# A hybrid attention and spectral-filter kernel: a short first chunk beside the front's last steps, the residual stored in raster order by ScalarE, and the chunks kept in written order

## The chip, the cores and the metric

The kernel runs on one core of one Trainium2 chip. The metric is the device time of one execution in microseconds (us). The engines are TensorE (PE, with PEld for its weight loads), VectorE (DVE), ScalarE (ACT), GpSimd (POOL) and SyncE (SP). SP only issues DMAs; ACT and POOL issue DMAs too, beside their other work.

## What is computed

The input is four images of 56 x 56 tokens with 128 channels, all in float32.

1. Layer 0: layer norm, 7 x 7 neighbourhood attention with four heads, projection with residual, layer norm, an MLP (128 to 512 to 128, GELU) with residual.
2. Layer 1, on the 3136 tokens of each image: a token-wise norm `t`, then `t + q * sum(k * v)`.
3. Layer 1, second half, on the norm `u` of that result: a residual plus a gated sum of spectral filters. Each filter is a causal convolution over tokens, followed by a 128 x 128 matrix per filter (16 filters, with and without an alternating sign), plus a short autoregressive part over three lags:

```python
U = irfft(rfft(phi) * rfft(u)); out = einsum('btkd,k,kde->bte', U_plus, s, Mpp)
out = out + einsum('btkd,k,kde->bte', U_minus, s, Mpm)     # filters
out = out + sum(u shifted by i @ Mu[i] for i in range(3))  # autoregressive part
```

The kernel does the convolution in the frequency domain with 8 x 245 frequencies: it transforms tokens to spectra, multiplies each frequency by a 128 x 128 matrix, and transforms back.

## The kernel before

The kernel has three stages that follow one another.

**The front** (to about 1255 us) takes the images in turn. The attention of image b (28 small tiles, `step`) is interleaved with the dense work of image b-1 (`finish_image`), by written costs: each `yield` names what a piece costs, and `dense` is advanced until a due amount is spent. The order on each engine's queue is that of the program text, since the whole front stands in `tc.manual_schedule()`. For the last image there is no attention left; its `finish_image` is interleaved only with `matrices`, which loads 32 blocks of filter matrices (512 KB each, line 992) and sums them into `mc`.

`finish_image` ends so: for each quarter j of the tokens, eight matmuls `px` (line 686) with wave tables `tab` (loaded by SP, line 298, five or ten ahead) give spectra, which DVE and POOL combine into `ab`; POOL stores `ab` to the scratch tensor `ud` (line 710). `last_steps` then does, for each of seven row groups g, `recent(g)` (the autoregressive part: matmuls `par`, line 628, and a DVE add into `x`, line 636) and `residual(g-1)` (four transposes `pf`, line 644, an ACT copy to `xf`, line 647, and four stores to `xd` from SP, line 650). For images 0 to 2 `last_steps` is spread over the quarters; for the last image all of it comes after them.

**The chunks** (about 1266 to 1816 us) multiply frequencies by matrices. There are 31 chunks of 8 x 8 frequencies; 245 = 30 x 8 + 5, so the last has five in place of eight. Chunk c needs

- `tokens(c)`: a 1 MB load `xc` from `ud` (line 1035), and 19 operations on POOL (`evens`, six; `odds`, ten; then two sums and a negation, lines 1047 to 1049) that make its spectra `v`. In chunk 0 the six evens are DVE's;
- `make(c, u)` for u = 0 to 7: 16 matmuls `pg` (line 1071, two records each) and four copies into the matrix tile `g` of 64 KB per partition, two on ACT (line 1082) and two on DVE (line 1084);
- `product(c, part)` for part = 0 to 7: matmuls `py` (line 1102) of `g` with `v`; after parts 1 and 5 ACT copies a sum to `ya`, after parts 3 and 7 DVE makes two `ys` and SP stores them to `yd` (line 1121).

The loop of chunk c alternates `make(c+1, u)` with `product(c, u)`. `xc`, `v` and `g` have two buffers each. This stage stands outside `manual_schedule`: the framework's scheduler orders the instructions of each queue by its own estimate of time. In the program that it made, SP's queue holds the `xc` loads of chunks 1, 2 and 3 ahead of chunk 0's stores, and from there on the load of chunk c+3 ahead of the stores of chunk c.

The pools of the chunks (`wg` with both `g`, `w3` with `xc`, `v` and the rest) are opened after `front.close()`, in the memory of the front.

**The back** (about 1808 to 2010 us) loads the products from `yd` into two `ring` tiles (in `g`'s buffers, 64 loads of 512 KB), combines them on DVE, multiplies them with inverse wave tables (`pi`, line 1219), adds the residual from `xd` and stores the result.

The lines by which the change can be followed: 101 (`qkv0`), 613 to 656 (`spread`, `recent`, `residual`, `last_steps`), 664 to 717 (`ab`, the quarters), 990 to 1025 (`matrices` and its interleaving), 1028 to 1169 (the chunks).

Of the kernel before, what the change touches and what calls it, by code (L numbers as in the profile page):

```python
# [25 lines left out]
GT = GR * W  # L26
QC = 14
# [22 lines left out]
NCH = -(-R // FC)  # L50
FB = 4
# [7 lines left out]
def conv_attn_hybrid_kernel(ctx: ExitStack, tc: tile.TileContext, a: dict, out: bass.AP):  # L59
# [11 lines left out]
    fp = front.enter_context(tc.tile_pool(name="front", bufs=1))  # L71
    attention = ExitStack()
# [4 lines left out]
    order = tc.manual_schedule()  # L77
    front.enter_context(order)
# [25 lines left out]
    qkv0 = load(fp, "qkv0", [C, 3 * C], a["w_qkv"], tag="xf", bufs=2)  # L104
# [84 lines left out]
    def setup_loads():  # L189
# [6 lines left out]
        late["fc10"] = load(fp, "fc10", [C, HID], a["w_fc1"], q, tag="xf", bufs=2)  # L196
# [4 lines left out]
        wl0 = fp.tile([C, 3, C], FP, tag="xf", name="wl0", bufs=2)  # L201
# [103 lines left out]
    def evens(eng, e, y, out):  # L305
        def all_of(v):
            last = " ".join("nf"[: len(v.shape) - 3])
            return v.rearrange(f"c p r {last} -> c (p r) {last}")

        eng.tensor_tensor(all_of(e[:, :2]), all_of(y[:, :2]), all_of(y[:, 2:]), ALU.add)  # L310
        eng.tensor_tensor(e[:, 2], y[:, 0], y[:, 2], ALU.subtract)
        eng.tensor_tensor(e[:, 3, 0], y[:, 3, 1], y[:, 1, 1], ALU.subtract)
        eng.tensor_tensor(e[:, 3, 1], y[:, 1, 0], y[:, 3, 0], ALU.subtract)
        if len(e.shape) > 4:
            e = e.rearrange("c p r n f -> c p r (n f)")
        eng.tensor_tensor(out[:, :2], e[:, ::2], e[:, 1::2], ALU.add)
        eng.tensor_tensor(out[:, 2:], e[:, ::2], e[:, 1::2], ALU.subtract)
# [181 lines left out]
    def finish_image(b, own=None):  # L499
# [118 lines left out]
        for r in range(2):  # L618
            spread(r, f"u{b}", rs, scale)
            yield 0.25  # L620
        def recent(g):
# [3 lines left out]
            for c0, c1 in zip(cuts, cuts[1:]):  # L625
# [9 lines left out]
            xg = raster(x[:, g])  # L635
            nc.vector.tensor_tensor(
                xg, ps[:, :GT].rearrange("c (h t w) -> c h t w", h=GR, t=NQ), xg, ALU.add
            )

        def residual(g):  # L640

            pf = ps_s.tile([TQ, NQ, C], FP, tag="s", name=f"pf_{b}_{g}")
            for t in range(NQ):
                nc.tensor.transpose(pf[:, t, :], x[:, g, t * TQ : (t + 1) * TQ], ident)
            tag, bufs = ("tok", 3) if own else ("xf", 2)
            xf = fp.tile([TQ, NQ, C], FP, tag=tag, name=f"xf_{b}_{g}", bufs=bufs)
            nc.scalar.copy(xf, pf)
            rows_of = xd[b].rearrange("(g h t w) c -> g t h w c", g=NG, h=GR, t=NQ)
            for t in range(NQ):
                nc.sync.dma_start(rows_of[g, t], xf[:, t, :])  # L650
# [14 lines left out]
        abs_of = (ab, own.tile([C, NCH, PH, 2 * FC], FP, name="ab2") if own else ab)  # L665
# [48 lines left out]
        if b == B - 1:  # L714
            yield from last_steps(range(NG))
# [264 lines left out]
    weighed = ExitStack()  # L980
    mpool = weighed.enter_context(tc.tile_pool(name="matrices", bufs=1, side="right"))
# [25 lines left out]

    with tc.tile_pool(name="last", bufs=1, side="right") as own, tc.tile_pool(
        name="weigh", bufs=1, side="right"
    ) as wp:  # L1010
        extra, due = matrices(wp), 0.0
        for spent in finish_image(B - 1, own):
            due += 0.4 * (spent if spent != "step" else 0.5)
            while due >= 1:
                next(extra, None)
                due -= 1
        run(extra)
    front.close()

    gpool = ctx.enter_context(tc.tile_pool(name="wg", bufs=2))
    with tc.tile_pool(name="w3", bufs=2) as wp, tc.tile_pool(
        name="ps_g", bufs=6, space=PSUM
    ) as ps_g, tc.tile_pool(name="ps_y", bufs=2, space=PSUM) as ps_y:
        filters_in, made, spectra, sums = {}, {}, {}, {}
        many = [min(FC, R - FC * c) for c in range(NCH)]

        def tokens(c):  # L1030


            n = NP * B
            x = wp.tile([C, n, CW], FP, tag="xc", name=f"xc{c}")
            (nc.sync if c else nc.gpsimd).dma_start(
                x, ud.rearrange("j b c w -> c (j b) w")[:, :, CW * c : CW * (c + 1)]
            )
            y = x.rearrange("c n (p r f) -> c p r n f", r=2, f=FC)
            v = wp.tile([C, 3, n * FC, PH], FP, tag="v", name=f"v{c}")
            w = v[:, 1:].rearrange("c r k m -> c m r k")  # L1040
            gp = nc.gpsimd
            ev = wp.tile([C, 4, 2, n, FC], FP, tag="od", name=f"ev{c}", bufs=1)
            evens(gp if c else nc.vector, ev, y[:, :4], w[:, :4])
            od = wp.tile([C, 3, 2, 2, n, FC], FP, tag="od", name=f"od{c}", bufs=1)
            odds(gp, od, y[:, 4:])
            od = od.rearrange("c i p r n f -> c i p r (n f)")
            gp.tensor_tensor(w[:, 4:6], od[:, 0], od[:, 2], ALU.add)
            gp.tensor_tensor(w[:, 6:], od[:, 0], od[:, 2], ALU.subtract)
            gp.tensor_scalar(v[:, 0], v[:, 2], -1.0, 1.0, ALU.mult, ALU.mult)
            spectra[c] = v  # L1050

        def filters_of(k):

            t = wp.tile([C, FB * CW], FP, tag="ph", name=f"ph{k}")
            n = min(FB, NCH - FB * k) * CW
            for rg in range(4):
                (nc.scalar if k else nc.gpsimd).dma_start(
                    t[32 * rg : 32 * rg + 32, :n], pd[:, FB * CW * k : FB * CW * k + n]
                )
            filters_in[k] = t  # L1060

        def make(c, u):

            if u == 0:
                made[c] = gpool.tile([C, CW, C], FP, tag="g", name=f"g{c}")
            g, t, at = made[c], filters_in[c // FB], c % FB * CW
            banks = [ps_g.tile([C, 4, CW], FP, tag="g", name=f"pg_{c}_{u}_{i}") for i in range(4)]
            for q in range(4):
                for rg in range(4):
                    r = slice(32 * rg, 32 * rg + 32)  # L1070
                    nc.tensor.matmul(  # L1071
                        banks[rg][:, q, :],
                        mc[r, 4 * u + q, :],
                        t[r, at : at + CW],
                        start=True,
                        stop=True,
                    )
            for rg in range(4):
                into = g[:, :, 32 * rg + 4 * u : 32 * rg + 4 * u + 4]
                src = banks[rg].rearrange("c q n -> c n q")  # L1080
                if rg % 2:
                    nc.scalar.copy(into, src)  # L1082
                else:
                    nc.vector.tensor_copy(into, src)  # L1084

        def weights(v, r, f, m):

            return v[:, r : r + 2].rearrange("c r (n f) m -> c f m (r n)", f=FC)[:, f, m]

        def product(c, part):  # L1090

            v, g = spectra[c], made[c]
            f0 = part // 4 * 4
            h, last = part // 2 % 2, min(many[c], f0 + 4)
            if part % 2 == 0:
                sums[0] = ps_y.tile([C, 4, C], FP, tag="y", name=f"py_{c}_{part}")
            py, f1 = sums[0], f0 + part % 2 * 2
            for f in range(f1, min(f1 + 2, last)):
                for r in range(2):
                    for m in range(4):  # L1100
                        slot = SLOTS.index(4 * h + m)
                        nc.tensor.matmul(  # L1102
                            py[32 * m : 32 * m + 32, f - f0, :],
                            weights(v, 1 - r, f, slot),
                            g[:, (2 * slot + r) * FC + f, :],
                            start=(r == 0),
                            stop=(r == 1),
                        )
            if part % 2 == 0:
                return  # L1110

            k = last - f0
            if h == 0:
                sums[1] = wp.tile([C, 4, C], FP, tag="ya", name=f"ya_{c}_{part}", bufs=1)
                nc.scalar.copy(sums[1][:, :k], py[:, :k])
                return
            for i, op in enumerate((ALU.add, ALU.subtract)):
                ys = wp.tile([C, 4, C], FP, tag=f"ys{i}", name=f"ys_{c}_{part}_{i}")
                nc.vector.tensor_tensor(ys[:, :k], sums[1][:, :k], py[:, :k], op)
                at = FC * c + f0  # L1120
                nc.sync.dma_start(yd[i, at : at + k, :C].rearrange("f q e -> q f e"), ys[:, :k])

        ring, ready, waves_back = [], {}, {}
        PAIR = 2 * B * C

        def ring_tile():
            name = f"ring{len(ring)}"
# [277 lines left out]
```

## Time and profile before

| | |
|---|---|
| median of 3 runs | 2007.86 us (2003.68 to 2009.82) |
| the profiled execution, its own time | 2011.93 us |
| its span | 2010.1 us |
| PE busy | 1854.4 us, 92% |
| DVE, ACT, POOL busy | 1201.5, 1029.0, 904.2 us |
| granted PE clock, mean | 0.953 |
| by stage, PE busy | 300 to 400: 92.95 of 100; 1260 to 1280: 10.62 of 20; 1400 to 1500: 100 of 100 |
| moved by DMA | 223.42 MB, mean 111 GB/s |

A line of the timeline gives start, duration, engine, source line, operation, output<-input tile, size and count; in square brackets stands the idle time before it and what ended it. "SPq" and "ACTq" are DMA issues on these engines' queues. A line of waits gives who waited for whom, the total, how often and the longest. A line of windows gives the stretch, then the busy time of PE, PEld, DVE, ACT and POOL, the granted PE clock, the busy share of the DMA engines and GB/s.

### The profile page before, as it was taken

The page shows a single profiled execution, that of the slowest core. Times are in us where ns is not written, and L with a number is a line of the kernel's source. Part 1 is how long each engine was busy: PE and PEld are TensorE (multiplying, and loading weights), DVE is VectorE, ACT ScalarE, POOL GpSimd, SP SyncE. Part 2 cuts the span into 40 slices and gives each one's busy share as a digit, 9 for nine tenths or more (in the row PEclk, how much of TensorE's full clock was granted, in tenths as well). Part 3 has the DMA queues.
Part 4 walks back from the last instruction along what each step waited for, and adds up shares of the span by engine and source line. Part 5 has one row for each costly group of instructions (what it writes and reads, how often), then busy time and mean ns, then how long its engine had stood idle before and what let it go on. Part 6 is the DMA issues. An engine that isn't in the chain of part 4 may idle for free.

```text
span 2010.1 us, 56713 instructions
## 1 busy us (share of the span) xinstructions
PE 1854.4 (92%) x23666; PEld 1172.5 (58%) x23666; DVE 1201.5 (60%) x2749; ACT 1029.0 (51%) x2311; POOL 904.2 (45%) x1446
## 2 busy tenths in 40 slices
PE   6899999998999988999998988699999999996998
PEld 3555554554554554554554434688888888882333
DVE  3676545454545554545555664577777777775883
ACT  1566685654686554685555333355555555550000
POOL 2444322564323463223473026588877777770000
PEclk8799999998999898999899989799999999997999
DMA  4140000153000252000254538344444444439991
GB/s 114 33 130 12 1 1 1 53 190 110 1 1 1 73 193 86 1 1 1 80 171 145 188 100 279 98 135 129 134 132 124 121 125 132 124 88 372 373 325 65
DMA packets 191389, 223.42 MB, mean 111 GB/s; under 512 B 12008, under 2 KB 171049, under 8 KB 188540
## 3 DMA queue, kind: packets, MB, share of 16 engines
q1 hardware_dynamic: 182992, 166.69, 27.3%
q0 software_dynamic: 2752, 34.33, 4.4%
q10 hardware_dynamic: 5388, 18.76, 2.6%
q8 instruction: 187, 3.06, 0.7%
q14 instruction: 70, 0.57, 0.1%
HBM read 141.77 MB, written 77.97 MB: 109 GB/s over the span
## 4 chain that ended last, share of the span: by engine, by line
PE 75%; issue 7%; DVE 6%; DMA 5%; ACT 4%; SPq 2%; POOL 1%; ACTq 0%; POOLq 0%; DVEq 0%
PE pg L1071 14%; PE py L1102 13%; PE pi L1219 7%; PE px L686 5%; PE ppt L794 4%; PE pl L738 4%; PE ph L537 3%; PE pf L528 3%; PE par L628 3%; PE pav L850 2%; PE pv L814 2%; DMA ring<-yd 2%; ACT p L765 2%; DVE p L751 2%; SPq L650 2%
## 5 line engine op out<-in xcount | busy, mean ns | idle before, releaser
L778 POOL TENSOR_SCALAR p<-p,den 112x280 f32<-112x280 f32 x448 | 214.9, 498 | 493.6 <-DVE den L776 264.9
L1084 DVE COPY g<-pg 128x512 f32<-128x512 f32 x496 | 319.5, 687 | 159.7 <-PE pg L1071 149.4
L1082 ACT COPY g<-pg 128x512 f32<-128x512 f32 x496 | 271.2, 602 | 235.7 <-PE pg L1071 228.6
L1071 PE MATMUL pg<-ph,mc 32*128 32x128 f32 x7936 | 298.9, 286 | 11.8 <-POOL od L326 5.1
L1071 PEld LDWEIGHTS pg<-ph,mc 32*128 32x128 f32 x7936 | 251.1, 189 | 52.7 <-issue 36.0
L765 ACT ACTIVATE p<-p,low 112x280 f32<-112x280 f32 x448 | 231.1, 517 | 92.3 <-DVE low L751 92.0
L1102 PE MATMUL py<-g,v 128*32 128x128 f32 x7840 | 275.2, 281 | 2.4 <-issue 2.0
L1102 PEld LDWEIGHTS py<-g,v 128*32 128x32 f32 x7840 | 219.1, 152 | 31.8 <-issue 2.9
L751 DVE CUSTOM_DVE_ANT_0 p<-pl,bias 112x280 f32<-112x280 f32 x448 | 174.7, 445 | 15.7 <-PE pl L738 3.5
L686 PE MATMUL px<-tab,tok 98*128 98x496 f32 x256 | 126.5, 638 | 21.0 <-DMA tab<-in_tab 14.1
L801 DVE COPY pt<-ppt 120x448 f32<-120x448 f32 x112 | 69.4, 620 | 117.4 <-PE ppt L794 116.5
L794 PEld LDWEIGHTS ppt<-ident,p 112*120 112x120 f32 x896 | 100.5, 139 | 59.4 <-issue 41.7
L794 PE MATMUL ppt<-ident,p 112*120 112x112 f32 x896 | 127.1, 263 | 5.7 <-DVE middle L836 4.3
L1219 PE MATMUL pi<-ring,io 128*98 128x512 f32 x256 | 112.9, 602 | 17.6 <-DVE ring L1181 15.5
L694 POOL TENSOR_TENSOR ab<-ab,w 128x496 f32<-128x496 f32 x60 | 74.5, 1242 | 108.4 <-ACT w L693 97.2
L801 ACT COPY pt<-ppt 120x448 f32<-120x448 f32 x224 | 87.1, 443 | 55.5 <-PE ppt L794 55.3
L537 PE MATMUL ph<-ln_m,w_fc 128*128 128x448 f32 x224 | 105.7, 564 | 4.7 <-DVE ln_m L518 4.6
L738 PE MATMUL pl<-kt,qt 32*112 32x280 f32 x896 | 94.0, 442 | 10.8 <-ACT qt L488 6.0
L545 ACT ACTIVATE h<-ph,b_fc 128x448 f32<-128x448 f32 x112 | 69.4, 633 | 61.8 <-PE ph L537 60.7
L528 PE MATMUL pf<-h,w_fc 128*128 128x448 f32 x224 | 101.0, 541 | 0.0
L686 PEld LDWEIGHTS px<-tab,tok 98*128 98x128 f32 x256 | 50.1, 207 | 79.3 <-issue 53.2
L1219 PEld LDWEIGHTS pi<-ring,io 128*98 128x98 f32 x256 | 42.6, 168 | 87.4 <-issue 80.9
(237 smaller groups left out, 3230.3 us busy)
## 6 DMA issues: line engine op xcount, KB each, us to landing
ring<-yd SPq DMA_DIRECT2D x64, 512.0 KB
ud<-ab POOLq DMA_DIRECT2D x16, 1984.0 KB, 7.1
yd<-ys SPq DMA_DIRECT2D x122, 256.0 KB
xc<-ud SPq DMA_DIRECT2D x30, 1024.0 KB
tab<-in_tab SPq DMA_DIRECT2D x160, 189.9 KB
mat<-in_M_phi_plus SPq DMA_DIRECT2D x16, 512.0 KB
mat<-in_M_phi_minus SPq DMA_DIRECT2D x16, 512.0 KB
x<-in_x SPq DMA_DIRECT2D x28, 224.0 KB
```

The lines of the kernel that those rows point to most:

```text
L537: nc.tensor.matmul(ph[:, :GT], w_fc1[:, i * C : (i + 1) * C], lnm[:, g * GT : (g + 1) * GT], start=True, stop=True,)
L686: nc.tensor.matmul(ps, toks[i // 4][:, i % 4, :], next(tab), start=True, stop=True)
L738: nc.tensor.matmul(pls[h][:TQ, :KEYS], qts[b, g][hs, t * TQ : (t + 1) * TQ], kt[hs, r0 : r0 + KR, c0 : c0 + KC], start=True, stop=True,)
L751: nc.vector.tensor_tensor_reduce(out=f["p"][:, h, :], in0=f["pls"][h][:TQ, :KEYS], in1=bias[:, h, :], scale=-1.0, scalar=3.0e38, op0=ALU.a ...
L765: nc.scalar.activation(f["p"][:, h, :], f["p"][:, h, :], AF.Exp, bias=f["low"][:, h : h + 1], scale=-1.0, accum_out=f["den"][:, h : h + 1],)
L778: nc.gpsimd.tensor_scalar(f["p"][:, h, :], f["p"][:, h, :], f["den"][:, h : h + 1], 1.0, ALU.mult, ALU.mult)
L794: nc.tensor.transpose(ppt[:, i, :], of, ident[:TQ, :TQ])
L1071: nc.tensor.matmul(banks[rg][:, q, :], mc[r, 4 * u + q, :], t[r, at : at + CW], start=True, stop=True,)
L1082: nc.scalar.copy(into, src)
L1084: nc.vector.tensor_copy(into, src)
L1102: nc.tensor.matmul(py[32 * m : 32 * m + 32, f - f0, :], weights(v, 1 - r, f, slot), g[:, (2 * slot + r) * FC + f, :], start=(r == 0), stop ...
L1219: nc.tensor.matmul(banks[j, p], it, z, start=(fh == 0 and k == 0), stop=(fh == 1 and k == len(of) - 1),)
```

## The change

- `residual(g)` no longer works on the (strip, row, column) order of `x`. `recent(g)` adds into a new tile `xr` in raster order (one of the three "t" buffers); `residual` transposes every fourth column of it, so that a partition of `xf` holds four tokens that follow each other, and one DMA from ACT's queue stores the group (2 KB per partition) in place of four from SP's. `xf` and the three weight tiles that shared its tag move to a pool `residual` of their own, opened after the front's; for the last image, too, it has two buffers (three of `tok` before).
- The three missing frequencies go to the first chunk in place of the last: chunk 0 uses frequencies 3 to 7 of its eight, `make(0, u)` computes 80 columns in place of 128, and `product` of the last chunk is full. The host's table is shifted to match.
- The pool of the chunks, `w3`, is opened on the right side, where `last` and `weigh` were, before the front's last steps of the last image. The filter load and `tokens(0)` are started there: `xc0` is loaded by SP in two parts (quarters 0 to 2, then 3), and DVE's evens are placed after `recent(5)` and `recent(6)`. DVE also takes one sum and the negation (in two parts) of chunk 0. The two `ab` tiles of the last image change places, so that the last quarter's is the front's.
- `g`'s two buffers become two pools of one buffer. `matrices` stays open to the end, and one inverse wave table of the back lies in `mc`.
- The last chunk's `ys` are stored by ACT in place of SP. `matrices` is advanced at 0.45 in place of 0.4 per unit of cost.
- `manual_schedule` now ends after the chunks: their instructions stand on each queue in the order of the program text.

The core of the diff:

```diff
+XQ = GT // TP
+SKIP = NCH * FC - R
...
+    res = front.enter_context(tc.tile_pool(name="residual", bufs=2))
...
-    order = tc.manual_schedule()
-    front.enter_context(order)
+    order = ExitStack()
+    order.enter_context(tc.manual_schedule())
...
+        xr = {}
+
         def recent(g):
...
-            xg = raster(x[:, g])
+            xr[g] = temp(f"xr_{b}_{g}")
             nc.vector.tensor_tensor(
-                xg, ps[:, :GT].rearrange("c (h t w) -> c h t w", h=GR, t=NQ), xg, ALU.add
+                xr[g].rearrange("c (h t w) -> c h t w", h=GR, t=NQ),
+                ps[:, :GT].rearrange("c (h t w) -> c h t w", h=GR, t=NQ),
+                raster(x[:, g]),
+                ALU.add,
             )
 
         def residual(g):
 
-            pf = ps_s.tile([TQ, NQ, C], FP, tag="s", name=f"pf_{b}_{g}")
-            for t in range(NQ):
-                nc.tensor.transpose(pf[:, t, :], x[:, g, t * TQ : (t + 1) * TQ], ident)
-            tag, bufs = ("tok", 3) if own else ("xf", 2)
-            xf = fp.tile([TQ, NQ, C], FP, tag=tag, name=f"xf_{b}_{g}", bufs=bufs)
+            pf = ps_s.tile([TP, XQ, C], FP, tag="s", name=f"pf_{b}_{g}")
+            for t in range(XQ):
+                nc.tensor.transpose(pf[:, t, :], xr[g][:, t::XQ], ident)
+            xf = res.tile([TP, XQ, C], FP, tag="xf", name=f"xf_{b}_{g}", bufs=2)
             nc.scalar.copy(xf, pf)
-            rows_of = xd[b].rearrange("(g h t w) c -> g t h w c", g=NG, h=GR, t=NQ)
-            for t in range(NQ):
-                nc.sync.dma_start(rows_of[g, t], xf[:, t, :])
+            nc.scalar.dma_start(
+                xd[b, g * GT : (g + 1) * GT].rearrange("(n t) c -> n t c", t=XQ), xf
+            )
             if b + 2 < B:
                 fetch(b + 2, [g])
...
-        abs_of = (ab, own.tile([C, NCH, PH, 2 * FC], FP, name="ab2") if own else ab)
+        abs_of = (own.tile([C, NCH, PH, 2 * FC], FP, name="ab2") if own else ab, ab)
...
         if b == B - 1:
+            yield "spectra"
             yield from last_steps(range(NG))
...
+        if c:
+            nc.sync.dma_start(x, src)
+        else:
+
+            nc.sync.dma_start(x[:, : n - B], src[:, : n - B])
+            nc.sync.dma_start(x[:, n - B :], src[:, n - B :])
+            yield
...
+        gp, other = nc.gpsimd, nc.gpsimd if c else nc.vector
...
+        yield from evens(other, ev, y[:, :4], w[:, :4])
+        yield
+        if c:
+            od = cp.tile(of, FP, tag=tag, name=f"od{c}", bufs=bufs)
+        odds(gp, od, y[:, 4:])
+        od = od.rearrange("c i p r n f -> c i p r (n f)")
+        other.tensor_tensor(w[:, 4:6], od[:, 0], od[:, 2], ALU.add)
+        gp.tensor_tensor(w[:, 6:], od[:, 0], od[:, 2], ALU.subtract)
+        for m in (slice(PH),) if c else (slice(4), slice(4, PH)):
+            other.tensor_scalar(
+                v[:, 0, :, m], v[:, 2, :, m], -1.0, 1.0, ALU.mult, ALU.mult
+            )
...
+        k, n = (FC - SKIP, 2 * PH * (FC - SKIP)) if c == 0 else (CW, CW)
+        of = t[:, at : at + CW]
+        if c == 0:
+            of = of.rearrange("k (x f) -> k x f", f=FC)[:, :, SKIP:]
...
+            (nc.scalar if c == NCH - 1 else nc.sync).dma_start(
+                yd[i, at + skip : at + 4, :C].rearrange("f q e -> q f e"), ys[:, skip:]
+            )
...
-        for spent in finish_image(B - 1, own):
-            due += 0.4 * (spent if spent != "step" else 0.5)
+        for spent in last:
+            if spent == "spectra":
+                break
+            due += 0.45 * (spent if spent != "step" else 0.5)
...
+    cp = chunks.enter_context(tc.tile_pool(name="w3", bufs=2, side="right"))
+    filters_of(0)
+    first = tokens(0)
+    next(first)
+    for n, _ in enumerate(last):
+        if n in (2 * NG - 5, 2 * NG - 3):
+            next(first, None)
+    run(first)
     front.close()
...
+    gpools = [ctx.enter_context(tc.tile_pool(name=f"wg{i}", bufs=1)) for i in range(2)]
+    ps_g = chunks.enter_context(tc.tile_pool(name="ps_g", bufs=6, space=PSUM))
+    ps_y = chunks.enter_context(tc.tile_pool(name="ps_y", bufs=2, space=PSUM))
+    for u in range(8):
+        make(0, u)
+    for c in range(NCH):
+        if c + 1 < NCH:
+            if (c + 1) % FB == 0:
+                filters_of((c + 1) // FB)
+            run(tokens(c + 1))
...
+        for u in range(8):
+            if c + 1 < NCH:
+                make(c + 1, u)
+            product(c, u)
+    chunks.close()
+    order.close()
...
-    full[..., :R] = tab
+    full[..., SKIP:] = tab
```

## The prediction, made before the change was run

> **What bounds the kernel now.** I read the windows by stage, then the order of PE's work at the seam between front and chunks, then the waits there, then one chunk on every queue. All times are of the profiled execution. Windows (PE, PEld, DVE, ACT, POOL busy; PEclk; DMA share; GB/s):
>
> ```profile
> 1260.00:1280.00 20.00, 10.62 (x136) 9.35 (x136) 6.81 (x12) 4.46 (x9) 16.85 (x26) 0.50 0.43 111
> 1400.00:1500.00 100.00, 100.00 (x2971) 86.90 (x2965) 73.33 (x118) 57.26 (x105) 79.76 (x109) 1.00 0.48 133
> ```
>
> In the chunks PE has no gap at all; a better order there can win nothing and can only lose. At the seam PE is half idle at half clock. PE's timeline there:
>
> ```profile
> 1254.43 0.60 PE L644 MATMUL pf<-ident,x 128*112 128x128 f32 x4
> 1259.86 1.10 PE L644 MATMUL pf<-ident,x 128*112 128x128 f32 x4 [4.83 <-DVE x L636]
> 1266.04 3.78 PE L1071 MATMUL pg<-ph,mc 32*128 32x128 f32 x48 [5.08 <-POOL od L326]
> 1273.71 3.78 PE L1071 MATMUL pg<-ph,mc 32*128 32x128 f32 x52 [3.89 <-ACT g L1082]
> ...
> 1288.04 1.16 PE L1071 MATMUL pg<-ph,mc 32*128 32x128 f32 x28 [0.57 <-DVE g L1084]
> 1289.13 1.12 PE L1102 MATMUL py<-g,v 128*32 128x128 f32 x32
> ```
>
> Waits at the seam (total, times, longest), and in the chunks:
>
> ```profile
> DVE g L1084 <- DMA xd<-xf: 10.3, 1, 10.3
> POOL v L316 <- PE py L1102: 84.5, 27, 3.5
> ```
>
> The first copy into `g0` waits for the residual stores, because `g0` lies where `xf` lay; SP issues the 28 stores until 1270.7. The second line is the important one: in the chunks POOL waits for PE, so spectra are made ahead of need. One chunk on POOL and SP:
>
> ```profile
> 1403.25 1.34 POOL L310 TENSOR_TENSOR ev<-xc 128x512 f32<-128x512 f32 x1
> ...
> 1409.15 1.33 POOL L316 TENSOR_TENSOR v<-ev 128x512 f32<-128x512 f32 x1 [3.05 <-PE py L1102]
> ...
> 1419.48 1.04 POOL L1049 TENSOR_SCALAR v<-v 128x1024 f32<-128x1024 f32 x1
> 1409.85 0.95 SPq L1121 DMA_DIRECT2D yd<-ys  x2
> 1414.93 0.36 SPq L1035 DMA_DIRECT2D xc<-ud  x1
> ```
>
> A chunk's last product ends at E = 1408.91. POOL then writes the `v` of two chunks on and is done at 1420.49, E + 11.6; PE wants it at E + 18.4 (a chunk of 17.3, (1807.8 - 1305.3)/29, and the 1.1 of one `pg` unit). Slack 6.8, only because `xc` was loaded and the first evens (1403.25 to 1406.05) done before E.
>
> [...]
>
> ```profile
> 1163.70:1165.60 1.90, 0.03 (x1) 0.00 (x0) 1.90 (x5) 0.00 (x0) 0.00 (x0) 1.00 0.91 262
> 1166.50:1169.50 3.00, 3.00 (x5) 1.33 (x4) 0.81 (x3) 0.63 (x1) 0.00 (x0) 0.50 1.03 270
> 1190.80:1194.30 3.50, 0.00 (x0) 0.00 (x0) 3.50 (x4) 0.00 (x0) 0.00 (x0) 0.89 0.00 0
> 1194.30:1200.20 5.90, 5.90 (x16) 3.78 (x17) 4.41 (x7) 1.17 (x2) 0.00 (x0) 0.50 0.00 0
> ```
>
> [...] The trace has data flowing 1.7 us after the issue at 1414.93, then 1.5 MB (with two stores) at 300 GB/s until 1421.6. [...]
>
> **The change, part by part.**
>
> *Seam.* Residual stores become one per group on ACT, out of a pool that `g0` does not cover; chunk 0's spectra start inside the last steps. `px` ends at 1236.1 and the seven `par`/`pf` rounds at 1255 as now; the last residual needs `xr` (0.62) and a transpose, PE free at about 1256.2, its copy done at 1256.9. The last `ud` store is issued at 1239.6 and lands 7.1 later (1247), so `xc0` is in by about 1251. DVE does the six evens (3.7), waits for POOL's odds (ten operations, 4.8, done 1255.6), then one sum (1.1) and two negations (some 0.6 each): free for `g0` at 1259.5. PE fills six banks, pauses about 1.5, then runs the other 6.5 units at 1.1 (80 columns in place of 128 make copies about 0.4, no longer the bound): chunk loop at 1267.2 against 1288.0 now. Chunk 0 has five frequencies: its first four units are bound by copies (1.75 each, as at 1284 to 1288), the others take 2.16: 15.6, E0 = 1282.8 against 1305.3, a gain of 22.5. The last chunk gets the three frequencies, 3.1 more, behind the 8 MB of `ring` loads, so hidden.
>
> *Written order in the chunks.* In the changed kernel as built, SP's order is: the two stores that end chunk c-1, then the `xc` of chunk c+1, then chunk c's stores. In the kernel before, the `xc` of a chunk stands a whole chunk earlier (first stores behind chunk 3's `xc`). So now nothing of chunk c+1 is loaded before E(c-1): DVE's two `ys` end at E + 1.5, SP has issued them at E + 1.9, then `xc`; its data flows from E + 3.6, where the stores' data end (2.8 us after the first issue at 1409.85); 1.05 MB at 330 GB/s is 3.2; landed and signalled E + 7.4. POOL's nineteen operations take 14.1 (2.8 + 2.6 + 4.8 + 2.7 + 1.0, and gaps), none before E any more. `v` is ready at E + 21.5, against E + 18.4: PE stands 3.2 us before the first `py`. Behind that `py` wait all later `pg` and `py`; the copies wait for those. From first `py` to the next end is 16.2 (17.3 less 1.1), so E(c+1) = E(c-1) + 37.8 to 37.9, not 34.6: a stall in each second chunk, 14 of them between E1 and E29. Each is longer than the gaps shown above, so I add the clock: 3.4 or 6.8 us at half rate cost 1.6 to 3.0 in the four such cases from 1091 to 1200; I take 2.3. E29 = 1282.8 + 17.3 + 14 x 40.2 = 1862.9 against 1807.8 now: +55, made of -22.5, 14 x 3.25 = 45.5 and 14 x 2.3 = 32.
>
> *Front, images 0 to 2.* Eighty-four stores (four per group) leave SP's queue, where they stand ahead of `tab` loads (0.63 issue each). PE waits 12.0 us for `tab` there (4.2, 5.7 and 2.1 in three images), with some 5 of slow clock behind. The image fetch remains on SP but waits only for DVE. Gain between 0 and 16; I take 12. ACT gains 21 issues; in the chunks an ACT copy beside such an issue took 0.68 in place of 0.59, and ACT is busy 60%: nothing, at worst 21 x 0.6 = 13 if each delayed PE. The strided transposes read a tile as `pt` does; the add writes elsewhere at the same 0.62; `matrices` at 0.45 moves loads earlier within the last image, at most 2.2 (its `tab` waits).
>
> *Back.* The first `pi` waits for the first eight `ring` loads after E29, as now. The last stores go out on ACT, so the second `ring` no longer waits from 1833.7 to 1839.1: PE's 2 us pause near 1861 goes. The last stores' data may delay the first `ring` by 1.4. I take -3, bounds -5 and +2.
>
> Sum: +55 - 12 - 3 = +40; span 2050 for 2010.1. The profiled run was 2011.9 and the median 2007.9; the shift is added to the median: 2048.
>
> **Rivals.** *A, the spectra are in time (faster).* Then E29 = 1282.8 + 29 x 17.3 = 1784.5, -23, and with front and back -38: 1970. It decides at one point: `xc` usable by E + 4.3. For it: if the copies drained faster than shown, or the hardware took the load early. Against: issue alone is at E + 1.9, and 1 MB in the 2.4 us left is over 430 GB/s with no latency[...].
> *B, the stall without the slow clock.* [...]+55 - 32 = +23, and with the rest +8: 2016. [...]against: all four gaps from 1.9 to 3.5 us were followed by half clock.
> *C, dearer stalls.* [...]`xc` a microsecond later, and no gain in the front: 14 x 1.1 = 15, and 12: 2075 to 2085. [...]
> *D, the seam doesn't shorten* (`xc0` as slow as today's 9.5, or `g0` still covered by a store): 7 to 22 later than the main case, 2055 to 2070.
>
> **How the numbers follow.** Main case 0.55 (its own range 2034 to 2062), A 0.06, B 0.14, C 0.15, D 0.1. Time 2048; leaving out A, half of B and the top of C gives 2018 to 2078. What a measurement of this kernel can tell from no change is 0.3%, 6 us. Faster: A and a tail of B, 0.08; same: B with the whole front gain, 0.04; slower: 0.88.
>
> **What would show it.** In the profile after: a row of PE waits, `py` released by POOL's negation of `v`, about 14, each near 3.2; POOL waiting for `xc` rather than PE; PEclk below 1 in the chunks; SP's `xc` behind the `ys` stores, 37 to 42 us per two chunks; first `pg` near 1257 (earlier by the front's gain), the `tab` waits gone. I am wrong if POOL still waits for `py`, or if the two-chunk period is 34.6.

## The result and the profile after

The changed kernel is slower: 2083.6 us, median of 4 runs (2079.9 to 2086.1), against 2008.1 for the kernel before on the same chip (2003.7 to 2009.8). The ratio is 1.0369, with a 95% interval of 1.0341 to 1.0397. I had forecast 2048 with a range of 2018 to 2078: the direction was right, the loss nearly twice as large as I said. The profiled execution has a span of 2084.0, against 2010.1: 73.9 to explain.

The page's fourth part, the chain that ended last, shows at once that PE has lost its hold on the end: PE had 75% of it before and POOL 1%.

```profile
PE 53%; POOL 20%; issue 14%; DVE 5%; DMA 4%; ACT 3%; ACTq 0%; SPq 0%; POOLq 0%; DVEq 0%
```

Windows of the changed kernel, the two stretches shown of the kernel before (PE, PEld, DVE, ACT, POOL busy; PEclk; DMA share; GB/s):

```profile
1260.00:1280.00 20.00, 18.85 (x316) 15.99 (x316) 9.60 (x18) 8.10 (x17) 2.51 (x3) 0.55 0.03 8
1400.00:1500.00 100.00, 93.72 (x2508) 79.49 (x2505) 61.41 (x97) 47.76 (x88) 67.89 (x94) 0.95 0.42 111
```

In the chunks PE ran 2508 matmul records in 100 us where it ran 2971. At the seam it is no longer idle, but at half clock: 94% busy at a granted 0.55.

I cut the span at points that both kernels have: the first `par` of the last image, E0 (the end of chunk 0's last product, where DVE's first `ys` of its second half starts), E29 (the same 29 chunks later) and the end.

| stretch | before | after | difference | forecast |
|---|---|---|---|---|
| start to the first `par` of the last image | 1235.95 | 1222.52 | -13.4 | -12 |
| from there to E0 | 69.6 | 63.9 | -5.7 | -22.5 |
| E0 to E29 | 502.5 | 589.8 | +87.3 | +77.5 |
| E29 to the end | 202.1 | 207.8 | +5.7 | -3 |
| sum | 2010.1 | 2084.0 | +73.9 | +40 |

Waits in the chunks of the changed kernel, 1300 to 1890 (total, times, longest):

```profile
POOL ev L314 <- DMA xc<-ud: 160.2, 27, 11.3
...
PE py L1115 <- POOL v L1052: 12.3, 18, 0.7
PE pg L1081 <- DMA ph<-pd: 10.9, 12, 2.1
PE py L1115 <- POOL v L1050: 8.3, 12, 0.8
...
PE py L1115 <- POOL v L1049: 5.3, 4, 2.5
...
PE py L1115 <- issue: 3.1, 4, 1.7
```

POOL waited for PE before (84.5 us, 27 times); now it waits for the token load, and PE waits for POOL. The third row I had not foreseen: PE also waits for `ph`, the filter load. One chunk in time order, on DVE, SP, POOL and PE. E, the end of the chunk's last product, is 1507.83 here; DVE's first `ys` starts 0.24 after it:

```profile
1508.07 1.27 DVE L1131 TENSOR_TENSOR ys<-ya,py 128x512 f32<-128x512 f32 x2
...
1509.84 0.50 SPq L1029 DMA_DIRECT2D xc<-ud  x1
...
1510.33 0.43 PE L1115 MATMUL py<-g,v 128*32 128x128 f32 x2 [0.80 <-POOL v L1050]
...
1511.46 0.91 PE L1115 MATMUL py<-g,v 128*32 128x128 f32 x24 [0.70 <-POOL v L1052]
...
1516.23 1.26 POOL L314 TENSOR_TENSOR ev<-xc 128x512 f32<-128x512 f32 x1 [4.82 <-DMA xc<-ud]
...
1529.44 1.05 POOL L1052 TENSOR_SCALAR v<-v 128x1024 f32<-128x1024 f32 x1
```

SP issues the load at E + 2.0, behind the two stores; it can be used at E + 8.4 (I had 7.4), POOL is done at E + 22.7 (I had 21.5). The two PE rows are the same wait one chunk earlier: PE starts on the slots that are ready and stands again for the next, so one lateness shows as two stands of 0.7 to 0.8.

PE at the seam:

```profile
1242.02 0.70 PE L654 MATMUL pf<-ident,xr 128*112 128x128 f32 x4 [0.42 <-DVE xr L643]
1246.35 1.57 PE L1081 MATMUL pg<-ph,mc 32*128 32x80 f32 x36 [3.63 <-POOL od L335]
1250.45 2.01 PE L1081 MATMUL pg<-ph,mc 32*128 32x80 f32 x32 [2.53 <-DVE g L1097]
1252.63 2.01 PE L1081 MATMUL pg<-ph,mc 32*128 32x80 f32 x32 [0.17 <-DVE g L1097]
...
1263.53 4.27 PE L1081 MATMUL pg<-ph,mc 32*128 32x80 f32 x64 [0.17 <-DVE g L1097]
```

The first `pg` comes near where I put it (1257 less the front's 12 is 1245; it is 1246.35). But each unit of chunk 0's filters then takes 2.18, not 1.1, and the first `py` follows at 1270.2.

### The profile page after: what moved, and what is told of

It reads as the page before. It is cut to its first block, busy times and chain, and to the rows that moved or that the text cites. A ratio compares the mean times of both kernels' runs of the same rounds, so it can differ in the third digit from the quotient of the medians.

```text
span 2084.0 us, 56616 instructions
## 1 busy us (share of the span) xinstructions
PE 1906.0 (91%) x23666; PEld 1209.0 (58%) x23666; DVE 1206.6 (58%) x2752; ACT 1024.4 (49%) x2311; POOL 901.6 (43%) x1439
## 3 DMA queue, kind: packets, MB, share of 16 engines
q1 hardware_dynamic: 169712, 160.53, 25.9%
## 4 chain that ended last, share of the span: by engine, by line
PE 53%; POOL 20%; issue 14%; DVE 5%; DMA 4%; ACT 3%; ACTq 0%; SPq 0%; POOLq 0%; DVEq 0%
PE pi L1264 7%; PE px L695 6%; PE ppt L804 4%; PE pl L748 3%; PE ph L542 3%; PE pf L533 3%; PE pg L1081 3%; PE par L635 2%; PE pav L860 2%; PE pv L824 2%; POOL v L321 2%; PE py L1115 2%; POOL v L1049 2%; POOL ev L314 2%; POOL v L322 2%
## 5 line engine op out<-in xcount | busy, mean ns | idle before, releaser
L1097 DVE COPY g<-pg 128x512 f32<-128x512 f32 (+1 forms) x496 | 318.9, 688 | 238.3 <-PE pg L1081 238.3
L1095 ACT COPY g<-pg 128x512 f32<-128x512 f32 (+1 forms) x496 | 264.3, 584 | 324.9 <-PE pg L1081 324.9
L1081 PE MATMUL pg<-ph,mc 32*128 32x128 f32 (+1 forms) x7936 | 324.3, 297 | 20.7 <-DMA ph<-pd 10.9
L1115 PE MATMUL py<-g,v 128*32 128x128 f32 x7840 | 300.7, 288 | 30.1 <-POOL v L1052 12.3
L1081 PEld LDWEIGHTS pg<-ph,mc 32*128 32x128 f32 x7936 | 271.9, 199 | 68.1 <-issue 48.0
L1115 PEld LDWEIGHTS py<-g,v 128*32 128x32 f32 x7840 | 230.5, 153 | 72.5 <-POOL v L1052 17.0
L761 DVE CUSTOM_DVE_ANT_0 p<-pl,bias 112x280 f32<-112x280 f32 x448 | 174.8, 445 | 16.2 <-PE pl L748 4.0
L314 POOL TENSOR_TENSOR ev<-xc 128x512 f32<-128x512 f32 x30 | 39.3, 1311 | 198.7 <-DMA xc<-ud 160.2
L748 PE MATMUL pl<-kt,qt 32*112 32x280 f32 x896 | 94.6, 444 | 10.9 <-ACT qt L493 6.0
L555 DVE SCALAR_TENSOR_TENSOR x<-pf,b_fc,x 128x448 f32<-128x448 f32 x28 | 19.1, 683 | 118.8 <-PE pf L533 118.8
```

Of the source, the lines that this page charges most:

```text
L748: nc.tensor.matmul(pls[h][:TQ, :KEYS], qts[b, g][hs, t * TQ : (t + 1) * TQ], kt[hs, r0 : r0 + KR, c0 : c0 + KC], start=True, stop=True,)
L761: nc.vector.tensor_tensor_reduce(out=f["p"][:, h, :], in0=f["pls"][h][:TQ, :KEYS], in1=bias[:, h, :], scale=-1.0, scalar=3.0e38, op0=ALU.a ...
L1081: nc.tensor.matmul(banks[rg][:, q, :n], mc[r, 4 * u + q, :], of[r], start=True, stop=True,)
L1115: nc.tensor.matmul(py[32 * m : 32 * m + 32, f - f0, :], weights(v, 1 - r, f, slot), g[:, (2 * slot + r) * FC + f, :], start=(r == 0), stop ...
```

## The experiments

All times are medians; each ratio is to the kernel before, run on the same chip beside the experiment. Its median was 2009.0 beside `e1` to `e4`, 2013.0 beside `e5`, `e6`, `e8` and `e9`, 2008.2 beside `e7` and `e10`, and 2007.2 beside `e11` and `e12`. Times inside an execution, as E0, come from the one profiled execution of each kernel.

**1. Two loads, one at a time and together.** Theory 1: the late token loads are most of the loss. Theory 2: it is the written order itself. Theory 3: the filter loads have an equal part. `e1_xc_early` issues the load of `xc` one chunk earlier, ahead of the stores:

```
...
+            if c == 0:
+                load_tokens(1)
             run(tokens(c + 1))
+            if c + 2 < NCH:
+                load_tokens(c + 2)
```

> The changed kernel with one edit: the token load of chunk c+2 is written after chunk c+1's spectra, so it stands ahead of chunk c's stores on SP's queue. Theory 1 (late loads behind the stores are most of the chunks' 87 us): POOL waits for py again, PE no longer waits for v, the chunk period falls from 20.3 to about 17.7; what is left is the filter loads' wait (10.9 us and some clock), so 2010 +- 8. Theory 2 (the written order of copies and matmuls, or the clock, costs by itself): within 15 of 2084. Theory 3 (the filter loads that PE waits for are an equal part): about 2040.

`e2_ph_early` loads the filters two chunks earlier:

```
-            if (c + 1) % FB == 0:
-                filters_of((c + 1) // FB)
+            if (c + 3) % FB == 0 and c + 3 < NCH:
+                filters_of((c + 3) // FB)
```

> The changed kernel with one edit: the filter load of four chunks is written two chunks earlier on ACT's queue. The 10.9 us of waits of pg for it must vanish in every theory. Theory 1: the token loads still set the period, part of the gain is absorbed: 2065 to 2080. Theory 3: 2045 or below. Theory 2: 2072 (the wait alone).

`e3_both_early` has both edits.

> Both loads early, all else as in the changed kernel. Theories 1 and 3: no stall in the chunks, period 17.3, PE clock 1.0 there: 87 us less, 1997 +- 6, faster than the kernel before by the front's 12 us and what the seam gains. Theory 2: 2070 or more.

Measured: 2061.1 (ratio 1.0267, 1.0231 to 1.0303), 2071.9 (1.0337, 1.0279 to 1.0395) and 2041.7 (1.0181, 1.014 to 1.0223). From 2083.6 the two edits win 22.5 and 11.7, and together 41.9. The filter loads alone won what Theories 1 and 2 both allowed, and Theory 3 is out. The other two runs fit no theory: Theory 1 wanted 2010 for the token load and 1997 for both, Theory 2 almost no gain. The mechanism of Theory 1 was removed all the same: with both edits POOL waits for PE again (131.5 us, 25 times, between 1300 and 1780), and PE waits for neither `v` nor `ph`. PE now stands for something else, once in nearly every chunk. Waits and PE's timeline of `e3_both_early`:

```profile
PE py L1124 <- issue: 24.6, 14, 2.1
PE pg L1090 <- issue: 7.0, 6, 1.6
```
```profile
1487.19 0.44 PE L1124 MATMUL py<-g,v 128*32 128x128 f32 x4 [1.60 <-issue]
...
1506.63 0.44 PE L1124 MATMUL py<-g,v 128*32 128x128 f32 x4 [1.75 <-issue]
```

"Issue" means that the profile shows nothing that PE waited for. The DMA view of the same kernel shows what moved: its queue table lists, beside q1, a queue q8 of the kind "instruction". These are its answers for 1477.5 to 1484.5, just ahead of the first stand, and for 1484.5 to 1485.0 (packets, MB, share of 16 engines):

```profile
q1 hardware_dynamic: 3105, 1.57, 87.5%
```
```profile
q8 instruction: 1, 0.02, 14.7%
q1 hardware_dynamic: 15, 0.00, 4.8%
```

One stretch of 5.75 us, 1478.75 to 1484.5, has the token load and two stores back to back, 1.57 MB, and no packet of q8; one packet of q8 comes as the data end, and PE's stand of 1.60 ends at 1487.19.

Neither the data nor the distance of q8's packets tells where PE stands. The kernel before has a stretch of 7.25 us of data (1485.0 to 1492.25, with a packet of q8 at 1489.0, 5.0 after the one before it) and no stand. In the changed kernel two packets of q8 are 7.5 apart (1507.75 and 1515.25), with 1.55 MB between them; PE waits 0.80 and 0.70 for `v` in that time, and behind the second packet nothing is put down to issue up to 1530. So what PE stood for in `e3` is not shown; that it has to do with the large load was my estimate, which the third experiment tries.

**2. The order alone, from both sides.** `e4_after_scheduled` closes the hand-written order ahead of the chunk loop, so that the scheduler orders the chunks as it did before:

```
+    order.close()
     for u in range(8):
         make(0, u)
     ...
     chunks.close()
-    order.close()
```

> The changed kernel with written order ended before the chunks, so that the scheduler orders them as in the kernel before. Theories 1 and 3: as with both loads early, 1997 +- 8, and the loads stand early on SP's queue. If the changed pools, the short chunk or the clock at the seam cost the 87 us: near 2084.

`e5_before_written` is the kernel before with its chunk loop in written order and nothing else changed: `order` becomes a stack of its own, as in the changed kernel, closed behind the loop.

> The kernel before with one thing changed: its chunk loop too is emitted in written order. Theory 'order' (the written order of the chunks is the whole loss, and the other parts of the change only gain): the chunks take as long as in the changed kernel, 85 us more than before, so 2085 to 2095; between 2070 and 2100 it stands. Rival 'mixture' (the loss needs the short first chunk, the new pools or the last stores on ACT as well): 2050 or less.

`e4`: 2017.7 (1.0044, 1.0028 to 1.0061). Within the changed kernel the order costs 66. It missed Theory 1's 1997: E0 to E29 takes 526.5, 24.0 more than before. Stands put down to issue are there too, up to 1.0 each, 10.4 in all. Another 12.0 is busy time of PE (514.3 for 502.3), which the profile does not explain. `e5`: 2101.7 (1.0424, 1.0383 to 1.0465). In the kernel before the order costs 88.7, and E0 to E29 takes 598.3, 95.8 more; the chunks of the changed kernel lost 87.3. Its waits from 1300 to 1780 are of the same kind as in the changed kernel:

```profile
POOL ev L310 <- DMA xc<-ud: 141.0, 20, 21.3
...
PE py L1102 <- POOL v L1049: 8.0, 14, 0.7
```

The rival, a loss that needs the mixture, is out for the chunks.

**3. The stands put down to issue: the load cut in four.** `e6_quarters` keeps the written order and both early loads, and cuts the token load into four of 256 KB, issued after parts 0, 2, 4 and 6 of the chunk:

```
+        for i in range(0, n, k):
+            nc.sync.dma_start(loaded[c][:, i : i + k], src[:, i : i + k])
+            yield
...
             product(c, u)
+            if u % 2 == 0:
+                next(pieces, None)
```

> The changed kernel in written order, with filter loads two chunks early and the token load of chunk c+2 cut into four quarters of 256 KB, spread over the parts 0, 2, 4 and 6 of chunk c, in place of one 1 MB load (2041.7 with both loads early and whole). Theory 'blocks' [...]: PE's stands put down to issue, 32 us in the chunks, fall under 6, and the time is 2012 +- 8. Rival 'order by itself' (PE stands for something that the written order of its own queue makes): the stands stay, 2035 or more.

Measured: 2000.1 (0.9938, 0.9916 to 0.996), 42 below `e3` and faster than the kernel before; the expectation said 2012. Its waits from 1300 to 1780, and its window 1400 to 1500:

```profile
PE py L1126 <- issue: 0.2, 1, 0.2
```
```profile
1400.00:1500.00 100.00, 99.92 (x2940) 86.65 (x2936) 72.70 (x115) 55.85 (x103) 81.26 (x112) 1.00 0.46 126
```

Stands of 31.6 us have become 0.2, and E0 to E29 takes 506.1 in place of 555.2 (the profiled execution of `e3` took 2051.6, 9.9 above its median). In `e6` the longest stretch of data from 1487 to 1500 is 4.5 us (1492.25 to 1496.75), where `e3` had 5.75. So the written order as such costs a chunk next to nothing (506.1 / 29 is 17.5, before 17.3); its loads did. The edit both shortens the stretches of data and spreads them, and no run takes one of the two alone; why PE stood is not shown.

**4. The residual part alone.** `e8_residual_alone` is the kernel before with only `recent` and `residual` changed and the pool for `xf`: the chunks, the first chunk's length, their pools and their order are those of before.

```
+            xr[g] = temp(f"xr_{b}_{g}")
...
-            for t in range(NQ):
-                nc.sync.dma_start(rows_of[g, t], xf[:, t, :])
+            nc.scalar.dma_start(
+                xd[b, g * GT : (g + 1) * GT].rearrange("(n t) c -> n t c", t=XQ), xf
+            )
```

> The kernel before with the residual part alone: residual in raster order in a pool of its own, one store per group from ACT; chunks, pools and order as before. Theory: the waits for tab go (-12) and the first copies into g0 no longer wait for 28 stores on SP (10.3 of DVE's wait, of which PE sees some 4 to 10): 1988 to 1996. Rival (the front's gain came with another part of the change): 2003 or more.

Measured: 1989.3 (0.9885, 0.9859 to 0.9912): 23.7 faster than the kernel before, and the fastest kernel of this study. The front gains 16.2 here (first `par` at 1219.71) and the seam 8.4 more (E0 is 24.7 earlier). The front's end varies by a few microseconds between kernels with the same front: it is 1222.5 in the changed kernel, 1219.6 in `e6` and 1224.9 in `e9`, and with the old front 1235.95 before and 1238.78 in `e5`. So 16.2 and 13.4 are not two different gains. Its PE timeline at the seam:

```profile
1244.97 1.11 PE L651 MATMUL pf<-ident,xr 128*112 128x128 f32 x4 [6.17 <-DVE xr L640]
1246.80 2.51 PE L1077 MATMUL pg<-ph,mc 32*128 32x128 f32 x36 [0.72 <-issue]
1249.84 2.09 PE L1077 MATMUL pg<-ph,mc 32*128 32x128 f32 x32 [0.53 <-DVE g L1090]
1252.30 1.77 PE L1077 MATMUL pg<-ph,mc 32*128 32x128 f32 x32 [0.37 <-DVE g L1090]
1254.65 1.17 PE L1077 MATMUL pg<-ph,mc 32*128 32x128 f32 x32 [0.58 <-DVE g L1090]
```

It begins chunk 0's filters at 1246.80, makes them for all eight frequencies, and reaches E0 at 1280.87, 5.5 ahead of the changed kernel, which makes five. Of the 5.5, 2.8 is the front's; counted from the first `par`, `e8` needs 61.2 and the changed kernel 63.9. So the short first chunk bought nothing at the seam. The next runs ask why.

**5. The seam: buffers, VectorE, or the short matmuls.** `e9_scheduled_xf4` (on `e4`) and `e7_quarters_xf4` (on `e6`) give the last image's residual copies four buffers, in a pool `more`:

```
-            xf = res.tile([TP, XQ, C], FP, tag="xf", name=f"xf_{b}_{g}", bufs=2)
+            pool, bufs = (more, 4) if own else (res, 2)
+            xf = pool.tile([TP, XQ, C], FP, tag="xf", name=f"xf_{b}_{g}", bufs=bufs)
```

> The changed kernel with scheduled chunks (2017.7 before this edit), and in the last image four buffers for the residual's copies in place of two. Theory 'two buffers' (PE's stand of 3.7 us after the last residual comes from copies that wait for stores to land[...]): 2007 +- 3. Rival 'engines' (VectorE and GpSimd, [...]release the first copies of chunk 0 no earlier[...]): 2014 to 2018.

> The changed kernel with the token loads in quarters and filters early (2000.1 before this edit), and four buffers for the last image's residual copies. The previous run with that edit moved PE's first stand into its second, where VectorE was at work on chunk 0's spectra. Theory 'VectorE holds the copies': nothing again, 2000 +- 4. Rival 'the buffers count once the chunks are clean': 1993 or less.

Measured: 2022.4 (1.0047, 1.003 to 1.0063; `e4` had 1.0044) and 2001.9 (0.9955, 0.9937 to 0.9973; `e6` had 0.9938). No gain: the theories in which the buffers count are out. PE's timeline of `e9` shows the first stand gone and the second grown to take its place, for the first copy still waits for DVE:

```profile
1245.78 1.34 PE L1082 MATMUL pg<-ph,mc 32*128 32x80 f32 x36 [0.76 <-POOL od L331]
1252.82 2.01 PE L1082 MATMUL pg<-ph,mc 32*128 32x80 f32 x32 [5.70 <-DVE g L1098]
```

DVE is held by POOL's odds and by its own sum and negations (1248.11 to 1252.3). The sum and the pair of negations take 2.12 and 2.29 there, and 1.10 and 2.84 in the changed kernel. `e10_negation_late` (on `e7`) writes the negations after the fourth unit of filters:

```
+        if c == 0:
+            yield
         for m in (slice(PH),) if c else (slice(4), slice(4, PH)):
...
         make(0, u)
+        if u == 3:
+            run(first)
```

> As the run beside it, and chunk 0's two negations on VectorE are written after the fourth unit of its filters, not ahead of the first copy. Theory 'VectorE holds the copies[...]': the second stand (2 to 5.7 us) shrinks below 1.5, the clock stays full, a unit of chunk 0's filters takes about 1.0 in place of 2.18, and the time falls by 8 to 13 against the run beside it, to 1987 to 1992. Rival 'half clock anyway' [...]: only the 2 to 3 us of the negations, 1996 to 1999.

Measured: 1999.0 (0.9951, 0.9932 to 0.997). The second stand fell from 5.26 in `e7` to 1.84 only, and the units still took 2.18 at half clock: the gain of 8 to 13 missed, and the number is the rival's upper end. This pointed at rows that I had read past. PE's groups of `e10` from 1247 to 1271 by form (times, busy, mean ns), and windows at its seam:

```profile
L1095 PE MATMUL pg<-ph,mc 32*128 32x80 f32 x256 | 16.5, 422 | 3.6 <-DVE g L1111 2.9 <-issue 0.7
L1095 PE MATMUL pg<-ph,mc 32*128 32x128 f32 x56 | 4.3, 442 | 0.5 <-DVE g L1111 0.4
```
```profile
1252.00:1258.00 6.00, 5.60 (x93) 5.17 (x96) 2.17 (x6) 1.64 (x4) 5.92 (x7) 0.50 0.02 4
1258.00:1264.00 6.00, 5.49 (x93) 4.85 (x92) 3.60 (x8) 2.46 (x6) 5.76 (x12) 0.50 0.02 4
1264.00:1269.50 5.50, 5.15 (x84) 4.34 (x80) 2.25 (x5) 2.06 (x5) 2.94 (x3) 0.50 0.01 3
```

A matmul of 80 columns took here what one of 128 took. At half clock 32 of them take 2.01 against 2.08; at full clock 36 take 1.34 (`e9`, at 1245.78, granted 1.00), 37 ns each, where 32 of 128 columns take 1.17, 37 ns each. And the granted clock is 0.50 from 1252 to 1269.5, with PE 93% busy, where the prediction had these units at full clock. `e11_full_columns` (on `e6`) and `e12_full_late` (on `e10`) make chunk 0's filters for all eight frequencies, with copies of 512; the products stay short:

```
-        k, n = (FC - SKIP, 2 * PH * (FC - SKIP)) if c == 0 else (CW, CW)
+        n = CW
         of = t[:, at : at + CW]
-        if c == 0:
-            of = of.rearrange("k (x f) -> k x f", f=FC)[:, :, SKIP:]
...
```

> The changed kernel with the token loads in quarters and filters early (2000.1), and the filters of chunk 0 made for all eight frequencies, as before the change: matmuls of 128 columns in place of 80, copies of 512 elements in place of 320; its products stay short. Theory 'short matmuls keep the clock down' (a matmul of 80 columns takes PE as long as one of 128, 63 ns at half clock[...]): the clock is back within 8 us of the first of these matmuls, by 1252 where it was 1271 to 1277, in spite of longer pauses; a unit takes 1.75 in place of 2.18; the chunks begin 4 to 7 earlier, 1994 to 1997. Rival 'pauses keep the clock down': half clock throughout, no gain or a loss, 2000 to 2004.

> The same edit, made on the kernel with four buffers for the last residual copies and chunk 0's negations written late (1999.0). Theory 'short matmuls keep the clock down': the clock returns within 8 us, 1990 to 1995. Rival 'pauses': 1999 or more.

Measured: 1995.5 (0.9943, 0.9922 to 0.9964) and 1994.8 (0.9944, 0.9927 to 0.996): 4.6 and 4.2 below their bases in microseconds, but the ratios to before can't tell them apart from theirs. The clock can. Windows at the seam of `e11`:

```profile
1248.00:1252.00 4.00, 2.73 (x44) 2.44 (x48) 2.73 (x5) 1.07 (x2) 3.92 (x5) 0.50 0.00 0
1252.00:1256.00 4.00, 2.88 (x72) 2.49 (x72) 2.47 (x4) 2.15 (x4) 3.84 (x9) 0.88 0.00 0
1256.00:1262.00 6.00, 4.26 (x124) 3.49 (x116) 4.17 (x8) 3.38 (x7) 4.70 (x6) 1.00 0.01 3
```

With longer pauses (0.37 to 0.57 against 0.17) and PE 52 to 72% busy from 1244 to 1256, the clock is full from about 1253 on, 9 us after the first of these matmuls, not the 8 I had written. The kernels with 80 columns have it back only 1.4 to 10 us after their first matmuls of 128 columns: in `e10` these begin at 1269.8 and the clock is full from 1271.2, in the changed kernel at 1268.2 and 1278.0. In `e3` PE has no pause above 0.17 from 1248.5 to 1268.8, all of 80 columns, and the clock reads 0.50 for all of it, so the rival of `e11` does not fit. The kernel before and `e8`, which also make 128 columns, agree: there the clock is full from about 1282.3 and 1253.6, 8.6 and 6.8 after PE's last pause of more than 0.6; in the changed kernel that took 27.6.

`e11` and `e12` change the copies too (512 elements for 320), so the columns are not varied quite alone. From the first `par` to E0 it is 58.3 in `e11`, 61.9 in `e6`. In `e12` the units slow down once more, from 1256.5 to 1260.6 (1.88 and 1.86 for 1.17; granted 0.72 from 1256 to 1262), behind a pause of 1.14 and with 128 columns. What sets the clock is not shown.

The stretches of the result's table in the runs that the account below uses:

| stretch | before | changed | `e4` | `e5` | `e6` | `e8` | `e11` |
|---|---|---|---|---|---|---|---|
| first `par` to E0 | 69.6 | 63.9 | 62.2 | 63.5 | 61.9 | 61.2 | 58.3 |
| E0 to E29 | 502.5 | 589.8 | 526.5 | 598.3 | 506.1 | 503.9 | 504.3 |
| E29 to the end | 202.1 | 207.8 | 202.6 | 202.4 | 208.7 | 202.0 | 208.7 |

## Why the prediction was wrong

**Chunks, the mechanism: right.** POOL waits for `xc`, PE for POOL, SP's load sits behind the `ys` stores, and PEclk is 0.95 (1400 to 1500). Undoing the order (`e4`) or making it alone (`e5`) moves 66 and 89 us, 63 and 96 of them in the chunks. The two-chunk period is 40.7 (twice 589.8 / 29), within the 37 to 42 that I gave.

**Chunks, the size: 87.3 for 77.5, near the sum but from wrong terms, which is luck in part.** I had 45.5 of stands (14 x 3.25) and 32 of slow clock. PE's busy time from E0 to E29 is 549.0, so it was idle 40.8: 25.9 for `v`, 10.9 for `ph`, 3.1 for issue, 0.4 for `g`. The other 46.5 is busy time above 502.5. A granted clock of 0.96 there accounts for some 22 of it, an estimate (549.0 x 0.04); which rows hold the rest the profile does not say. The lateness was split into 34 short waits (at most 2.5; two that make 1.5 in the chunk shown), rather than 14 of 3.2. The load was also a microsecond later than in my chain (E + 8.4 for 7.4).

**A step that was missing: the filter loads.** "Of a step that is moved" I followed `xc` and not `ph`. `filters_of` is written at the head of the chunk whose `make` reads it at once, and in written order its four loads have no time: 10.9 us of PE, and 11.7 in the experiment that moves only them.

**Seam: -5.7 where I had -22.5. This is the largest error, 17 us.** The failed step is "then runs the other 6.5 units at 1.1 (80 columns in place of 128 make copies about 0.4, no longer the bound)". It puts the slow clock at nothing, right behind a pause of PE's own. In the kernel before, PE's four pauses of 3.4, 2.6, 1.9 and 3.5 us (up to 1094.5, 1153.6, 1165.6 and 1194.3) each came with a granted 0.50, from within the pause or at most 0.6 behind it, for 3.4, 6.7, 3.4 and 6.8 us; the last two are in the prediction's windows. The 1.1 is no saving by the shorter matmul: it is what 32 of 128 columns take at full clock (1.17). But the pauses were 3.63 and 2.53, where I had 0.8 (1256.2 to 1257) and about 1.5, and the clock stayed at a half until 1278, eight microseconds into chunk 0's own products. It took 23.8 from the first `pg` (1246.35) to the first `py` (1270.18), where I had 11.3 (1267.2 + 1.1 - 1257): 12.5 of the 17. Most of the rest is ahead of it: from the first `par` to the first `pg` it took 23.8, where 1257 - 1235.95 is 21.1.

Which part brought the -5.7 is open. The residual's pool and store alone, with a full first chunk, gain 8.4 here (`e8`). But the kernel before in written order, with none of the new parts, gains 6.1 too (`e5`). The early spectra show 2.9 over `e8` where the columns are full (58.3 for 61.2, `e11`), and nothing in `e4` and `e6`, with 80 columns.

**Front: right**, -13.4 for -12; the `tab` waits of 12.0 are gone.

**Back: +5.7 for -3.** PE's first `pi` rows, before and after (each second row runs to the edge of its window):

```profile
1831.25 29.65 PE L1219 MATMUL pi<-ring,io 128*98 128x512 f32 x64 [15.49 <-DVE ring L1181]
1862.95 20.54 PE L1219 MATMUL pi<-ring,io 128*98 128x512 f32 x46 [2.06 <-DVE ring L1180]
```
```profile
1902.12 29.66 PE L1264 MATMUL pi<-ring,mc 128*98 128x512 f32 x64 [16.27 <-issue]
1935.78 15.67 PE L1264 MATMUL pi<-ring,io 128*98 128x512 f32 x32 [4.00 <-DVE ring L1226]
```

Having seen SP's order for `xc`, I did not apply it to `ring`. In written order its loads start behind the stores of E29, at E29 + 2.9, where before the first went out at E29 itself. The first `pi` comes at E29 + 25.9, before at 23.2, and the pause at the second `ring`, which I said would go, is 4.0 in place of 2.1. The longer last chunk is hidden under the scheduler's order, as forecast: the changed kernel with scheduled chunks (`e4`) has 202.6 from E29 to the end, with a first load at E29 itself and the first `pi` at E29 + 23.9; `e9`, scheduled too, has 201.9. So the loss goes with the written order. It needs the changed end of the chunks as well, for the kernel before in written order (`e5`) has 202.4. Putting the chunks' own loads right does not help: `e6` has 208.7. Which of the parts of that end (the full last chunk, its stores on ACT, the wave table in `mc`) it takes, no run separates.

**The rivals.** A (spectra in time) is out; it takes other places for the loads in the written order (`e6`) to get there. B (no slow clock) is out: the clock is 0.96 from E0 to E29. C, with 2075 to 2085, named the time and not the reason: its dearer stalls came, but part of its sum was the front's gain failing, and that gain came. D, a seam that does not shorten, was true for a cause that it did not list. I let the rivals happen one at a time. What happened was my case with dearer stalls and a seam that did not shorten, together, and the range left no room for both.

## What to carry to other kernels

When the order of a loop is fixed by hand, follow every load in it, the small and rare ones too, to its place in its queue: in one queue a prefetch written behind a store that waits for the end of the iteration is no prefetch. Here POOL waited 160.2 us for such loads in the changed kernel's chunks, and PE 10.9 for the filters. Four small loads spread over an iteration beat one large early one (2000.1 against 2041.7). Where PE stands for "issue" in the chunk loop, try the large load beside it in pieces: here that took 31.6 us of stands to 0.2. Before pricing a shorter matmul, look for a row of that shape, and for the clock beside it: here 37 ns for 80 columns and for 128 at full clock.

## What the hardware showed that I had not expected

- A matmul of 32 rows and 80 columns took no less than one of 32 rows and 128: 37 ns each at a granted 1.00 (`e9`, `e11`), 63 and 65 at 0.50 (the changed kernel, `e11`).
- With those matmuls the granted clock was 0.50 to their end, 17 us in `e10` and 20 in `e3`, with PE over 90% busy; with 128 columns and PE 52 to 72% busy it was 1.00 again 9 us after the first one (`e11`). Why is not shown.
- In `e3` PE stood 1.60 us behind 5.75 us in which 1.57 MB had moved without a break. A stretch of 7.25 us of data made no stand in the kernel before. With the 1 MB load in four, the stands put down to issue in the chunks were 0.2 in place of 31.6 (`e6`, `e3`).
- Where DVE and POOL were both at work on the spectra of chunk 0, single instructions took longer: in the changed kernel POOL's difference (L1050) took 2.06 at 1246.27, with DVE's sum and negations beside it, and 1.29 at 1260.18 and at 1508.99. DVE's sum took 1.10 there and 2.12 in `e9`. No run takes one of the two engines away, so the cause is not shown.
